# Gated units of a fused decoder kernel: token shift in the columns of the turned rows, with row statistics passed on by small transfers

## The chip, the core and the metric

The kernel is one launch on one core of a Trainium2 chip. Its metric is the device time of the launch in microseconds (us), lower is better. A core has a matrix engine (TensorE, PE in the views; its weight loads are PEld), a vector engine (VectorE, DVE), a scalar engine (ScalarE, ACT), a general engine (GpSimd, POOL) and a queue engine (SyncE, SP) that issues nearly all transfers of this kernel. Each engine takes its instructions in order and waits on semaphores for what other engines and transfers produce. A matmul contracts over the 128 partitions of its two operands in SBUF and writes to a bank of PSUM, which VectorE and ScalarE read.

## The reference, cut to what matters

A decoder of two layers on an input of 8 x 512 x 256 in float32: self-attention, cross-attention, a stage "ffn" of two local-attention layers with gated units, then quantised attention, media attention and experts. The change concerns the gated units, the second half of each of the two layers of the "ffn" stage:

```python
def shift_token(t):
    t1, t2 = jnp.split(t, 2, axis=-1)
    t2 = jnp.pad(t2, ((0, 0), (1, 0), (0, 0)))[:, :-1]
    return jnp.concatenate([t1, t2], axis=-1)
...
    x = x + o @ wo
    h = shift_token(x)
    mu = h.mean(-1, keepdims=True)
    var = h.var(-1, keepdims=True)
    h = (h - mu) / jnp.sqrt(var + 1e-05) * lg + lb
    h = h @ w1 + b1
    a, g = jnp.split(h, 2, axis=-1)
    h = a * jax.nn.gelu(g, approximate=False)
    x = x + h @ w2 + b2
```

So row t of h has channels 0 to 127 of row t and channels 128 to 255 of row t - 1 (zero for the first row of a sequence). The layer normalisation runs over this mixed row. The inner width of the unit is 682.

## The kernel before, in words

**Layout.** x stays in SBUF for the whole kernel as 128 partitions x 32 tiles x 256 channels. One of the 8 sequences ("block" b) is four tiles of 128 rows: row 128 i + p of the sequence lies in partition p of tile i. A shift by one row is therefore a shift by one partition, with a step from partition 127 of tile i - 1 to partition 0 of tile i.

**Stages and who puts them in order.** Each stage is a Python generator or function that records instructions. A generator of class Ahead yields between pieces of its preparation, and the stage before it calls ahead.step() in its last rounds, so that preparation of the next stage is recorded among them. local_attention (L1758) does so for local_ffn: one step at its start, one in each of its last seven rounds, and a last call that takes the rest up to "yield Ahead.MAIN". After recording, a scheduler puts the instructions of every engine in an order by their priority and by when it expects their inputs; it can move work ahead of what was recorded before it, within the limits of the tile pools (a tag with bufs=2 has two buffers, and a third user waits for the first to be released).

**local_ffn (L2015), before the change.** At its start it builds two 128 x 128 matrices, shift and carry (L2027 to L2031), by GpSimd selections: shift has ones where a column is the partition plus one, carry a single one from partition 127 to partition 0. Then, for a block:

- shifted(b), L2043: two matmuls (L2049 with shift, 512 columns, L2050 with carry, 384 columns) write the shifted upper channels of the four tiles to a bank; ScalarE copies it to lf_h (L2051). ln_stats (L134; L142, L143) runs BN statistics over the lower half of x and over lf_h, and one aggregation for the pair; rsqrt (L1455 to L1463) makes the inverse root in ten small VectorE instructions on 128 x 4 values. normalize (L154, L156) writes hn, eight instructions of 128 x 128.
- turned(b), L2060: eight PE transposes (L2066) put the channels on the partitions; VectorE scales each half with gain and bias of the layer normalisation from PSUM into hnT (L2069), 128 x 512 each.
- chunk(b, f), L2079, six times: matmuls with w1 for the gate and the other factor (up, L2073), Gelu on ScalarE (L2096, lf_gate), and the product on VectorE (L2100, lf_hid or lf_tail). The sixth chunk is the narrow tail.
- then, for each of four row tiles, six matmuls with w2 (L2143) and the sum into x (L2148). In the second layer GpSimd adds the residual (L2150) and finished(b) takes row statistics for the next stage.

Block 0's shifted, turned and chunks are recorded before MAIN, that is, in the end of local_attention. In the main part shifted(b + 1) is recorded at f = 0 of block b, turned(b + 1) at f = 3. Every matmul of float32 appears as two instructions in the trace, so the 2 of a shift are 4 rows.

**The neighbours.** The end of local_attention is a round trip: masks on VectorE (L1928, la_e), exponentials on ScalarE (L1932), products on PE (L1939, banks po and sum), a copy la_o (L1961, three buffers). The sums go to DRAM and back spread over the partitions (sums L3111, x_sums L3112), are inverted (L3115), go to DRAM (L3116) and come back wide (x_wide, L3128, four transfers); GpSimd multiplies (L3129, la_oT), and the output projection follows on PE (L1987) with the sum into x on VectorE (L1992). All of these transfers are issued by SP, in order.

Of the kernel before, what the change touches and what calls it, by code (L numbers as in the profile page):

```python
# [27 lines left out]
F32 = mybir.dt.float32  # L28
# [5 lines left out]
ALU = mybir.AluOpType  # L34
# [4 lines left out]
P = 128  # L39
B, S, C = 8, 512, 256  # L40
NST = S // P
NT = B * NST
EPS = 1e-5
# [12 lines left out]
class Decoder:  # L56
# [35 lines left out]
    def bank(self, tag):  # L92

        return self.alloc(self.psum, [P, 512], F32, tag)
# [1182 lines left out]
class FastDecoder(Decoder):  # L1277
# [737 lines left out]
    def local_ffn(self, l, y, ahead):  # L2015

        nc, t = self.nc, self.t
        w1, w2 = self.load_local_ffn(l)
        last = l == 1
        yield  # L2020
        with self.tc.tile_pool(
            name="lf", bufs=2, reuse_waits="tile", side="left" if last else "right"
        ) as pool:

            shift = self.alloc(pool, [P, P], F32, "lf_shift", bufs=1)
            carry = self.alloc(pool, [P, P], F32, "lf_carry", bufs=1)
            for m, step, base, mul in ((shift, 1, -1, -1), (carry, -P, 1 - P, 1)):  # L2027
                nc.gpsimd.affine_select(
                    out=m, in_=self.ones, pattern=[[step, P]], compare_op=ALU.is_equal, fill=0.0,
                    base=base, channel_multiplier=mul,  # L2030
                )  # L2031
            gb = self.alloc(pool, [P, 4], F32, "lf_gb", bufs=1)
            b1 = self.alloc(pool, [P, 2 * NHC - 1], F32, "lf_b1", bufs=1)
            nc.sync.dma_start(gb, t["c_ln"][l])
            nc.sync.dma_start(b1, t["c_b1"][l])

            tails = []
            for j in range(2):
                tails.append(self.alloc(pool, [64, S], F32, f"lf_tail{j}", bufs=1))
                nc.gpsimd.memset(tails[j][32:64, :], 1.0)  # L2040
            held = {}

            def shifted(b):  # L2043

                d = held[b] = {}
                h = self.alloc(pool, [P, NST, P], F32, "lf_h")
                ps = self.pj()
                rows = y[:, b * NST : (b + 1) * NST, :]
                nc.tensor.matmul(ps, shift, rows[:, :, P:], start=True, stop=False)  # L2049
                nc.tensor.matmul(ps[:, P:], carry, rows[:, : NST - 1, P:], start=False, stop=True)  # L2050
                nc.scalar.copy(h.rearrange("p t c -> p (t c)"), ps)  # L2051
                stats = self.ln_stats(pool, lambda i: [rows[:, i, :P], h[:, i, :]], NST, "lf_ln")
                hn = d["hn"] = self.alloc(pool, [P, NST, C], F32, "lf_hn")
                for i in range(NST):
                    self.normalize(hn[:, i, :P], rows[:, i, :P], stats, i)
                    self.normalize(hn[:, i, P:], h[:, i, :], stats, i)
                if last:
                    d["x"] = self.residual(pool, b)

            def turned(b):  # L2060
                d = held[b]
                hnT = d["hnT"] = self.alloc(pool, [P, 2, S], F32, "lf_hnT")
                for c in range(2):
                    ps = self.pj()
                    for i in range(NST):
                        nc.tensor.transpose(  # L2066
                            ps[:, i * P : (i + 1) * P], d["hn"][:, i, c * P : (c + 1) * P], self.ident
                        )
                    nc.vector.tensor_scalar(  # L2069
                        hnT[:, c, :], ps, gb[:, c : c + 1], gb[:, 2 + c : 3 + c], ALU.mult, ALU.add  # L2070
                    )

            def up(ps, b, at, m):  # L2073
                for k in range(2):
                    nc.tensor.matmul(  # L2075
                        ps[:m, :], w1[:, k, at : at + m], held[b]["hnT"][:, k, :], start=(k == 0), stop=(k == 1)
                    )

            def chunk(b, f, bank):  # L2079

                d = held[b]
                if f == 0:
                    d["hid"] = self.alloc(pool, [P, NHC - 1, S], F32, "lf_hid")
                last_f = f == NHC - 1
                m, at = (TAIL, 64) if last_f else (P, 0)
                pa = bank("sc")
                if last_f:
                    up(pa, b, 2 * (NHC - 1) * P, PAIR)
                    pg = pa
                else:  # L2090
                    pg = bank("pj")
                    up(pg, b, (NHC - 1 + f) * P, P)
                    up(pa, b, f * P, P)
                col = 2 * NHC - 2 if last_f else NHC - 1 + f
                gate = self.alloc(pool, [P, S], F32, "lf_gate")
                nc.scalar.activation(  # L2096
                    gate[:m, :], pg[at : at + m, :], AF.Gelu, bias=b1[at : at + m, col : col + 1]
                )
                col = 2 * NHC - 2 if last_f else f
                nc.vector.scalar_tensor_tensor(  # L2100
                    tails[b % 2][:m, :] if last_f else d["hid"][:, f, :],
                    pa[:m, :], b1[:m, col : col + 1], gate[:m, :], ALU.add, ALU.mult,
                )

            yield
            shifted(0)
            yield
            turned(0)
            for f in range(NHC):
                yield  # L2110
                chunk(0, f, lambda tag: self.pj())
            yield Ahead.MAIN
            with self.banks():
                self.pj = lambda: self.bank("tr")
                order = ("pj", "sc", "po", "tr") if last else ("sc", "tr", "pj", "po")
                self.reserve(self.psum, *((tag, [P, 512], 2) for tag in order))
                if last:
                    self.integers = ExitStack()
                    self.qpool = self.integers.enter_context(
                        self.tc.tile_pool(reuse_waits="tile", name="qw", bufs=1, side="right")  # L2120
                    )
                    self.q = {"stats": [], "xtop": self.alloc(self.qpool, [P, NT], F32, "qw_xtop")}
                    self.w_quantized = self.load_quantized_attention()
                ahead.step()
                for b in range(B):
                    for f in range(NHC):
                        if b:
                            chunk(b, f, self.bank)
                        if b + 1 < B:
                            if f == 0:  # L2130
                                shifted(b + 1)
                            if f == 3:
                                turned(b + 1)
                        if b >= B - 2:
                            ahead.step(2)
                    if last and b == 1:
                        self.integer_weights(self.qpool, self.w_quantized)
                    for i in range(NST):
                        ps = self.bank("po")
                        for f in range(NHC):  # L2140
                            last_f = f == NHC - 1
                            src = tails[b % 2][: TAIL + 1, :] if last_f else held[b]["hid"][:, f, :]
                            nc.tensor.matmul(  # L2143
                                ps[:, :C], src[:, i * P : (i + 1) * P], w2[: src.shape[0], f, :],
                                start=(f == 0), stop=last_f,
                            )
                        yt = y[:, b * NST + i, :]
                        nc.vector.tensor_tensor(yt, yt, ps[:, :C], ALU.add)  # L2148
                        if last:
                            nc.gpsimd.tensor_tensor(yt, held[b]["x"][:, i, :], yt, ALU.add)  # L2150
                    if last:
                        self.finished(b)
                ahead.step(100)
# [1232 lines left out]
```

## Time and profile before

| | us |
|---|---|
| median of 3 runs | 3223.38 (3217.72 to 3229.64) |
| the profiled execution | 3223.79 |
| its span in the trace | 3222.1 |
| PE matmul of the shift, L2049, one of 32 instructions (28 of them, 4 others 0.644) | 0.592 |
| PE matmul of the carry, L2050, one of 32 instructions | 0.486 |
| copies lf_h on ScalarE, L2051 (16 of 0.586), together | 9.4 |
| VectorE waits for x_sums (L3115, 23 of 78), together | 35.9 |

The profile is of one execution. In its page, section 2 cuts the span into 40 equal slices (80.6 us each), a digit being the busy share in tenths. Durations of matmuls are longer than the distance between their starts, since matmuls are pipelined: what an instruction costs on PE is read from start to start. In a timeline the columns are start, duration (of a merged group: from first start to last end), engine, line, operation, output and inputs, shapes and count; a bracket holds the idle time before and what ended it.

### The profile page before, as it was taken

The page shows a single profiled execution, that of the slowest core. Times are in us where ns is not written, and L with a number is a line of the kernel's source. Part 1 is how long each engine was busy: PE and PEld are TensorE (multiplying, and loading weights), DVE is VectorE, ACT ScalarE, POOL GpSimd, SP SyncE. Part 2 cuts the span into 40 slices and gives each one's busy share as a digit, 9 for nine tenths or more (in the row PEclk, how much of TensorE's full clock was granted, in tenths as well). Part 3 has the DMA queues.
Part 4 walks back from the last instruction along what each step waited for, and adds up shares of the span by engine and source line. Part 5 has one row for each costly group of instructions (what it writes and reads, how often), then busy time and mean ns, then how long its engine had stood idle before and what let it go on. Part 6 is the DMA issues. An engine that isn't in the chain of part 4 may idle for free. (4 is left out here: it accounts for less than half of the span.)

```text
span 3222.1 us, 40035 instructions
## 1 busy us (share of the span) xinstructions
PE 2949.9 (92%) x15008; PEld 1504.2 (47%) x15008; DVE 2143.2 (67%) x4766; ACT 1154.4 (36%) x1607; POOL 410.2 (13%) x383
## 2 busy tenths in 40 slices
PE   8998798878998999999988989999797899997998
PEld 5642222224554555555455546554444233333665
DVE  7458888887887854366788777656788866566110
ACT  2146566643434331123434431112255334442111
POOL 1111001000110110000011011011302122222111
PEclk9999999988999999999999999999898999998999
DMA  7011111101000000000000011001232122222431
GB/s 232 1 58 45 58 53 39 39 17 53 15 21 15 21 28 34 1 1 34 15 21 21 22 41 59 14 14 59 61 141 97 52 67 93 80 73 87 117 135 58
DMA packets 125921, 168.41 MB, mean 52 GB/s; under 512 B 47158, under 2 KB 74893, under 8 KB 123670
## 3 DMA queue, kind: packets, MB, share of 16 engines
q1 hardware_dynamic: 121622, 154.17, 14.9%
q0 software_dynamic: 4096, 11.59, 1.0%
q8 instruction: 120, 1.97, 0.3%
q14 instruction: 83, 0.68, 0.1%
HBM read 112.95 MB, written 47.50 MB: 50 GB/s over the span
## 5 line engine op out<-in xcount | busy, mean ns | idle before, releaser
L1811 PE MATMUL pj<-w,la_hT 128*128 128x512 f32 x720 | 348.6, 617 | 25.6 <-DVE la_v L1816 23.9
L1663 DVE TENSOR_TENSOR x_e<-x_e,x_share 128x1024 f32<-128x1024 f32 x256 | 307.1, 1245 | 24.0 <-ACT x_e L1662 23.2
L1662 ACT ACTIVATE x_e<-sc 128x1024 f32<-128x1024 f32 x256 | 249.7, 1026 | 145.2 <-PE sc L1651 143.6
L2758 ACT ACTIVATE ma_e<-sc,ma_bias 128x1024 f32<-128x1024 f32 x128 | 142.6, 1115 | 198.6 <-PE sc L2753 185.4
L1811 PEld LDWEIGHTS pj<-w,la_hT 128*128 128x128 f32 x720 | 130.3, 192 | 169.2 <-issue 120.0
L3129 POOL TENSOR_TENSOR la_oT<-la_o,x_wide 128x512 f32<-128x512 f32 x64 | 97.5, 1534 | 799.1 <-DMA x_wide<-invs 459.1
L1932 ACT ACTIVATE la_e<-la_e 128x1024 f32<-128x1024 f32 (+1 forms) x128 | 121.5, 951 | 184.0 <-DVE la_e L1928 184.0
L2096 ACT ACTIVATE lf_gate<-pj,lf_b 128x512 f32<-128x512 f32 (+1 forms) x82 | 56.4, 687 | 358.4 <-PE pj L2075 358.4
L2766 DVE TENSOR_TENSOR ma_esum<-ma_esum,ma_e 128x1024 f32<-128x1024 f32 x96 | 122.9, 1281 | 91.7 <-ACT ma_e L2758 91.1
L2075 PE MATMUL pj<-lf_hnT,w 128*128 128x512 f32 (+1 forms) x368 | 173.5, 598 | 0.0
L1678 PE MATMUL po<-x_e,x_v 128*32 128x512 f32 x1024 | 139.9, 619 | 36.2 <-DVE x_e L1663 32.9
L1928 DVE TENSOR_TENSOR la_e<-sc,la_mask 128x1024 f32<-128x1024 f32 (+1 forms) x128 | 138.4, 1082 | 44.5 <-PE sc L1921 44.5
L1651 PE MATMUL sc<-x_q,x_k 32*128 32x512 f32 x1024 | 158.3, 658 | 0.3 <-ACT x_e L1662 0.2
L2075 PE MATMUL sc<-lf_hnT,w 128*128 128x512 f32 x336 | 155.9, 592 | 0.0
L2143 PE MATMUL po<-w,lf_hid 128*128 128x256 f32 x640 | 153.9, 386 | 0.0
L2753 PE MATMUL sc<-ma_qT,ma_kT 64*128 64x512 f32 x512 | 144.9, 643 | 0.0
L1987 PE MATMUL pj<-w,la_oT 128*128 128x256 f32 x512 | 124.3, 389 | 21.7 <-ACT la_qkT L1857 12.6
L2776 PE MATMUL po<-ma_e,ma_v 128*64 128x512 f32 x512 | 138.1, 618 | 0.0
L1921 PE MATMUL sc<-la_qkT 64*128 64x256 f32 (+1 forms) x1024 | 135.8, 384 | 0.0
L2143 PEld LDWEIGHTS po<-w,lf_hid 128*128 128x128 f32 x640 | 117.3, 190 | 34.6 <-issue 20.4
L1939 PE MATMUL po<-la_e,la_v 128*64 128x256 f32 (+1 forms) x1024 | 129.2, 373 | 3.4 <-ACT la_o L1961 3.4
L1818 ACT ACTIVATE la_sq<-pj 128x512 f32<-128x512 f32 x120 | 71.5, 596 | 156.2 <-PE pj L1811 156.1
(491 smaller groups left out, 5233.9 us busy)
## 6 DMA issues: line engine op xcount, KB each, us to landing
x_wide<-invs SPq DMA_DIRECT2D x184, 128.0 KB
w<-in_f_w_dram SPq DMA_DIRECT2D x16, 1024.0 KB
kv<-kv_o SPq DMA_DIRECT2D x56, 256.0 KB
slots<-x_empty SPq DMA_DIRECT2D x8, 1028.0 KB
x_mask<-in_x_maskT_dram SPq DMA_DIRECT2D x8, 1024.0 KB
ma_kT<-kv SPq DMA_DIRECT2D x8, 1024.0 KB
ma_v<-kv SPq DMA_DIRECT2D x8, 1024.0 KB
ex_rows<-slots SPq DMA_DIRECT2D x7, 1028.0 KB
```

Source lines behind the costliest of these rows:

```text
L1651: nc.tensor.matmul(pair[r // 2][:, r % 2, :], d["k"][rows, g, kt * P : (kt + 1) * P], d["q"][rows, e, g, :], start=True, stop=True,)
L1662: nc.scalar.activation(ex, d["e"][rest][p], AF.Exp)
L1663: nc.vector.tensor_tensor(ex, ex, d["share"][:, kt, :].unsqueeze(1).broadcast_to([P, 2, 512]), ALU.mult)
L1678: nc.tensor.matmul(d["po"][32 * r : 32 * r + 32, :], d["v"][:, kt, 8 * g + 2 * r + e, :], ex[r // 2][:, r % 2, :], start=(kt == 0), stop=( ...
L1811: nc.tensor.matmul(ps, d["hT"][:, k, i * P : (i + 1) * P], wqkv[:, k, j * S : (j + 1) * S], start=(k == 0), stop=(k == 1),)
L1921: nc.tensor.matmul(ps[:, r, jj * 256 : jj * 256 + to - j * P], d["qkT"][rows, 4 + c, j * P : (j + 1) * P], d["qkT"][rows, c, j * P : to], ...
L1928: nc.vector.tensor_tensor(ex[:, :, :n_cols], ps[:, :, :n_cols], mask[:, :n_cols].unsqueeze(1).broadcast_to([P, 2, n_cols]), ALU.add,)
L2075: nc.tensor.matmul(ps[:m, :], w1[:, k, at : at + m], held[b]["hnT"][:, k, :], start=(k == 0), stop=(k == 1))
L2143: nc.tensor.matmul(ps[:, :C], src[:, i * P : (i + 1) * P], w2[: src.shape[0], f, :], start=(f == 0), stop=last_f,)
L2753: nc.tensor.matmul(ps[:, r, :], d["k"][rows, c, kt * P : (kt + 1) * P], d["q"][rows, c, :], start=True, stop=True,)
L2758: nc.scalar.activation(ex, ps, AF.Exp, bias=bias[:, b * NST + kt : b * NST + kt + 1], scale=0.125)
L2776: nc.tensor.matmul(d["po"][64 * r : 64 * r + 64, :], d["v"][:, kt, 128 * c + 64 * r : 128 * c + 64 * r + 64], ex[:, r, :], start=(kt == 0) ...
```

## The change

The shift moves from the rows to the columns. The rows of the lower and upper channels are normalised where they lie, unshifted, each with the scale and offset of the mixed row that it will belong to, and the upper half is shifted by one column when the turned rows are scaled out of PSUM into hnT. For that, statistics are taken for each half alone (two aggregations for what was one), the upper half's mean and variance are sent one partition on (before), both are combined to the mixed row's mean and variance, and the scale and offset of a row (own) are sent one partition back (next) for the upper half. Each of these is a pair of transfers from SBUF to SBUF, one of 127 partitions x 8 values and one that carries partition 127 to partition 0 or back. shifted(b) becomes three pieces, halves, scales and normal, recorded at f = 0, 1 and 2 of the block before, with turned at f = 4 rather than 3; for block 0 each piece has a yield.

```diff
-            shift = self.alloc(pool, [P, P], F32, "lf_shift", bufs=1)
-            carry = self.alloc(pool, [P, P], F32, "lf_carry", bufs=1)
-            for m, step, base, mul in ((shift, 1, -1, -1), (carry, -P, 1 - P, 1)):
-                nc.gpsimd.affine_select(
...
+            befores, owns, nexts = [], [], []
+            for j in range(2):
+                befores.append(self.alloc(pool, [P, NST, 2], F32, f"lf_before{j}", bufs=1))
+                nc.gpsimd.memset(befores[j], 0.0)
+                owns.append(self.alloc(pool, [P, NST + 1, 2], F32, f"lf_own{j}", bufs=1))
+                nc.gpsimd.memset(owns[j], 0.0)
+                nexts.append(self.alloc(pool, [P, NST, 2], F32, f"lf_next{j}", bufs=1))
             held = {}
 
-            def shifted(b):
+            def halves(b):
 
                 d = held[b] = {}
-                h = self.alloc(pool, [P, NST, P], F32, "lf_h")
-                ps = self.pj()
-                rows = y[:, b * NST : (b + 1) * NST, :]
-                nc.tensor.matmul(ps, shift, rows[:, :, P:], start=True, stop=False)
-                nc.tensor.matmul(ps[:, P:], carry, rows[:, : NST - 1, P:], start=False, stop=True)
-                nc.scalar.copy(h.rearrange("p t c -> p (t c)"), ps)
-                stats = self.ln_stats(pool, lambda i: [rows[:, i, :P], h[:, i, :]], NST, "lf_ln")
+                rows = d["rows"] = y[:, b * NST : (b + 1) * NST, :]
+                mv = d["mv"] = self.alloc(pool, [P, 2, NST, 2], F32, "lf_mv")
+                for j in (1, 0):
+                    for i in range(NST):
+                        st = self.alloc(pool, [P, 6], F32, "lf_bn", bufs=4)
+                        nc.vector.bn_stats(st, rows[:, i, j * P : (j + 1) * P])
+                        nc.vector.bn_aggr(mv[:, j, i, :], st)
+                    if j:
+                        before = befores[b % 2]
+                        nc.sync.dma_start(before[1:], mv[: P - 1, 1])
+                        nc.sync.dma_start(before[0:1, 1:], mv[P - 1 :, 1, : NST - 1])
+
+            def scales(b):
+
+                mv, before, own, next_ = held[b]["mv"], befores[b % 2], owns[b % 2], nexts[b % 2]
+                total = self.alloc(pool, [P, NST, 2], F32, "lf_total")
+                apart = self.alloc(pool, [P, NST], F32, "lf_apart")
+                rstd = self.alloc(pool, [P, NST], F32, "lf_rstd")
+                nc.vector.tensor_tensor(total, mv[:, 0], before, ALU.add)
+                nc.vector.tensor_tensor(apart, mv[:, 0, :, 0], before[:, :, 0], ALU.subtract)
+                nc.vector.scalar_tensor_tensor(apart, apart, 0.5, apart, ALU.mult, ALU.mult)
+                nc.vector.tensor_tensor(apart, apart, total[:, :, 1], ALU.add)
+                nc.vector.tensor_scalar(apart, apart, 0.5, EPS, ALU.mult, ALU.add)
+                self.rsqrt(pool, rstd, apart, "lf_t")
+                nc.vector.tensor_copy(own[:, :NST, 0], rstd)
+                nc.vector.scalar_tensor_tensor(
+                    own[:, :NST, 1], total[:, :, 0], -0.5, rstd, ALU.mult, ALU.mult
+                )
+                nc.vector.tensor_copy(own[:, NST, 1:2], own[:, 0, 1:2])
+                nc.sync.dma_start(next_[: P - 1], own[1:, :NST])
+                nc.sync.dma_start(next_[P - 1 :], own[0:1, 1:])
+
+            def normal(b):
+                d = held[b]
                 hn = d["hn"] = self.alloc(pool, [P, NST, C], F32, "lf_hn")
-                for i in range(NST):
-                    self.normalize(hn[:, i, :P], rows[:, i, :P], stats, i)
-                    self.normalize(hn[:, i, P:], h[:, i, :], stats, i)
+                for j, (part, to) in enumerate(((slice(0, P), owns), (slice(P, C), nexts))):
+                    for i in range(NST):
+                        to_ = to[b % 2][:, i]
+                        nc.vector.tensor_scalar(
+                            hn[:, i, part], d["rows"][:, i, part], to_[:, 0:1], to_[:, 1:2],
+                            ALU.mult, ALU.add,
+                        )
...
-                    nc.vector.tensor_scalar(
-                        hnT[:, c, :], ps, gb[:, c : c + 1], gb[:, 2 + c : 3 + c], ALU.mult, ALU.add
-                    )
+                    pieces = (((0, S), (0, S)),) if c == 0 else (((1, S), (0, S - 1)), ((0, 1), (S - 1, S)))
+                    for (lo, hi), (lo_, hi_) in pieces:
+                        nc.vector.tensor_scalar(
+                            hnT[:, c, lo:hi], ps[:, lo_:hi_], gb[:, c : c + 1], gb[:, 2 + c : 3 + c],
+                            ALU.mult, ALU.add,
+                        )
...
             yield
-            shifted(0)
+            halves(0)
+            yield
+            scales(0)
+            yield
+            normal(0)
             yield
             turned(0)
...
-                            if f == 0:
-                                shifted(b + 1)
-                            if f == 3:
-                                turned(b + 1)
+                            if f in (0, 1, 2, 4):
+                                (halves, scales, normal, None, turned)[f](b + 1)
```

In the built program VectorE has 11 instructions more for each of the 16 blocks, SP 64 transfers more in all, PE and ScalarE have the shift's matmuls and copies fewer, and the orders of the engines differ from the first local attention's end on to the end of the second layer's gated units. What is recorded after that stands in the same order on PE.

More of the change, by code (lines that the diff above doesn't have):

```diff
@@ L2023, in local_ffn @@
         ) as pool:
-            shift = self.alloc(pool, [P, P], F32, "lf_shift", bufs=1)
-            carry = self.alloc(pool, [P, P], F32, "lf_carry", bufs=1)
-            for m, step, base, mul in ((shift, 1, -1, -1), (carry, -P, 1 - P, 1)):
-                nc.gpsimd.affine_select(
-                    out=m, in_=self.ones, pattern=[[step, P]], compare_op=ALU.is_equal, fill=0.0,
-                    base=base, channel_multiplier=mul,
-                )
             gb = self.alloc(pool, [P, 4], F32, "lf_gb", bufs=1)
@@ L2068, in turned @@
                         )
-                    nc.vector.tensor_scalar(
-                        hnT[:, c, :], ps, gb[:, c : c + 1], gb[:, 2 + c : 3 + c], ALU.mult, ALU.add
-                    )
+                    pieces = (((0, S), (0, S)),) if c == 0 else (((1, S), (0, S - 1)), ((0, 1), (S - 1, S)))
[4 more added lines that the diff above has]
+                        )
             def up(ps, b, at, m):
```

## The prediction

> **What bounds the kernel now.** I read the page first (shares, then the slices), then a table of windows cut at the stage borders, then the timeline of TensorE, VectorE and SP in those windows.
>
> ```profile
> PE 2949.9 (92%) x15008; PEld 1504.2 (47%) x15008; DVE 2143.2 (67%) x4766; ACT 1154.4 (36%) x1607; POOL 410.2 (13%) x383
> PE   8998798878998999999988989999797899997998
> DVE  7458888887887854366788777656788866566110
> ...
> 1140.00:1201.00 61.00, 55.85 (x334) 28.76 (x333) 33.66 (x70) 19.74 (x27) 10.23 (x10) 0.92 0.11 32
> 1201.00:1216.00 15.00, 14.90 (x67) 12.36 (x66) 4.09 (x9) 0.68 (x1) 2.54 (x3) 1.00 0.00 1
> 1216.00:1400.00 184.00, 184.00 (x590) 103.19 (x590) 76.21 (x272) 24.81 (x37) 0.00 (x0) 1.00 0.05 15
> 1880.00:1939.00 59.00, 53.22 (x334) 27.52 (x333) 33.93 (x70) 19.67 (x27) 10.14 (x10) 0.97 0.16 50
> 1954.00:2180.00 226.00, 225.35 (x736) 126.72 (x735) 150.05 (x539) 30.20 (x45) 24.26 (x31) 1.00 0.10 31
> ```
>
> Columns of the windows: stretch, its length, busy us (count) of PE, PEld, DVE, ACT, POOL, then granted clock, DMA share, GB/s. Seen over the whole span PE is only 92% busy, but in the two gated-unit stages (1216 to 1400, 1954 to 2180) it is busy without a gap at full clock, while VectorE is at 41% and 66%. In those stages a PE instruction removed is time removed. In the ends of the two local attentions before them (1140 to 1201, 1880 to 1939) PE stands 5.2 and 5.8 us.
>
> The timeline of one block of rows:
>
> ```profile
> 1266.28 1.02 PE L2049 MATMUL tr<-x,lf_shift 128*128 128x512 f32 x2
> ...
> 1297.76 1.88 PE L2075 MATMUL sc<-lf_hnT,w 128*128 128x512 f32 x4
> 1299.47 1.02 PE L2049 MATMUL tr<-x,lf_shift 128*128 128x512 f32 x2
> 1300.33 0.81 PE L2050 MATMUL tr<-x,lf_carry 128*128 128x384 f32 x2
> 1300.98 1.88 PE L2075 MATMUL pj<-lf_hnT,w 128*128 128x512 f32 x4
> ```
>
> Start to start (durations overlap in the pipeline): the shift takes 1299.47 to 1300.33, the carry to 1300.98, together 1.51 us; the period of a block is 1299.47 - 1266.28 = 33.19 us, all of it PE. That is the part that the change removes.
>
> At the attention's end the block's first rows are on the path instead:
>
> ```profile
> 1164.21 0.49 DVE L142 BATCH_NORM_STATS2 lf_ln_bn<-lf_h 128x6 f32<-128x128 f32 x2 [2.10 <-ACT lf_h L2051]
> 1173.36 1.22 DVE L1928 TENSOR_TENSOR la_e<-sc,la_mask 128x1024 f32<-128x1024 f32 x1
> ...
> 1168.30 1.08 PE L1939 MATMUL po<-la_e,la_v 128*64 128x256 f32 x8 [0.38 <-ACT la_o L1961]
> 1171.70 1.63 PE L2066 MATMUL pj<-ident,lf_hn 128*128 128x128 f32 x5 [2.31 <-DVE lf_hn L156]
> ...
> 1170.24 0.52 SPq L3111 DMA_DIRECT2D sums<-la_total  x1
> 1171.94 0.32 SPq L3112 DMA_DIRECT2D x_sums<-sums  x1
> ```
>
> PE waits 2.31 us for the normalised rows (2.26 in two waits in layer 1). Two SP lines give the price of a small transfer: x_sums waits for sums, 1171.94 - 1170.24 - 0.52 = 1.2 us after its issue ended, so some 1.7 us from issue to landing.
>
> **What the Trainium skill says.** "DMA: Bandwidth & Descriptors", section "Anatomy of one DMA", gives about 2.0 us fixed per transfer, most of it the write receipt; the 1.7 us above agrees, though that page fits another issuing path. "VectorE: DVE Perf Modes", section "The TRN2 errata", says that operands read from SBUF cost a fixed extra per instruction; the trace shows it, 0.15 to 0.16 us for four elements per partition. "SBUF — State Buffer", section "SBUF: two separate sides", says of the port pair shared by VectorE and GpSimd that it is an exclusive lock. This fits L148 at 1166.41, 1.25 us long instead of 0.16 beside a GpSimd product.
>
> **The change part by part.**
>
> *Removed, TensorE.* 16 blocks (8 rows of the batch, 2 layers), each shift and carry: 16 x 1.51 = 24.2 us. Of these 14 lie in the windows with a solid PE (21.1 us, taken in full) and 2 in the attention ends (3.0 us).
>
> *Removed, ScalarE.* 16 copies of 0.586 us (L2051). ScalarE is 13% busy in the stage: nothing, except that in the attention end the chain matmul, copy, statistics becomes statistics alone.
>
> *VectorE, per block.* Before: 8 BN statistics, 4 aggregations, 2 copies, 10 of the root, 8 normalisations, 2 turned scalings. After: 8, 8, 5 sums, 10, 3 for own, 8, 3 scalings. So 4 aggregations (0.192 us), 6 small ones (0.155) and the one-column piece (0.15, by the small ones) more: 1.85 us, 30 us in all. In the solid stages this lies in VectorE's idle time (59% and 34%). The one tight place there is the order transposes, scalings, normalisations, tail product: by starts, 0.9 us for the transposes, 1.72 for the last up matmuls and 2.25 for five down matmuls leave 4.85 us; VectorE needs 0.8 + 2 x 0.75 + 0.1 + 4 x 0.26 + 0.66 = 4.1. It fits, with 0.7 to spare.
>
> *Transfers.* Four per block on SP, 64 in all, about 0.35 us of issue each (x_sums' 0.32), 22 us of an idle queue. Two waits per block are added on VectorE: the sums wait for before, the second half of the normalisation for next. In the built order of instructions next is issued a block ahead of its use in the stages, some 30 us for a transfer of 1.7; so the price there is 0. Behind a wait stand masks, exponent inputs and gate products on VectorE, so it is not 0 in the attention ends.
>
> *Moved.* Since the statistics no longer need TensorE, the built order puts those of blocks 1 to 6 (7's too, in part) into the attention's end and the up matmuls beside it. Chunks of block 0 also start two steps later, since the preparation has two yields more; they still stand ahead of the output projection and fill the same wait. Between two gate products VectorE now has about 6 statistics pairs (0.26 us, start to start), 16 small ones (0.06 to 0.2 apart, I take 0.12) and the product (0.66): 4.1 us against 3.43 us of PE for a chunk. Over four chunks and two layers that is at most 5.6 us; the two banks take up part, and I charge 3. On SP the wide copies of the inverse sums now queue behind transfers that wait for VectorE, in layer 1 also behind four bias loads (about 0.45 us each by L2204's issues). I follow this by hand to 3 to 5 us later for the first pair; la_o has three buffers, so PE can wait there (0.38 before). Against it stand the 2.31 and 2.26 us waits that go, and masks that come up to 4 us earlier because the copy is gone. These bounds are -4 (gain) to +8 (loss) over both ends; I take +2 less the 3.0 for the removed pair, so the two ends together gain 1.
>
> *Setup.* Two selections per layer go, four memsets come (0.49 us each at most, on an idle GpSimd): 0.
>
> Sum: 21.1 + 1 = 22 us. The profiled execution took 3223.79 us (span 3222.1), less 22 gives 3201.8; the median shown is 0.4 lower. I say **3202**.
>
> **The rivals.**
>
> *A, VectorE takes over the attention ends* (chance 0.20). The gate products come late in each of the eight chunks, by up to 0.7 + 0.5 us of small operations spaced 0.15 apart, and two or three small-transfer waits fall on VectorE at the mean of the 23 waits that L3115 has now (35.9 / 23 = 1.56 us). For: six blocks of 8 pairs (2.1 us) and 18 small ones (2.2) are 26 us of new VectorE work there, in windows with 27 and 25 us idle. Against: most of it is placed where VectorE now waits for PE. Loss 10 us more: 3212, inside the uncertainty.
>
> *B, slower: SP's order holds up the attention's end* (0.07). A transfer on SP waits for VectorE's own; the wide copies of the inverses stand behind it; so GpSimd's product, the la_o buffers and PE wait, and with them the masks. Three rounds in each of two ends; the gain is eaten from 3.7 us a round (22 / 6), and slower by 0.5% from 6.4. At 7 us a round: 3223.8 - 22 + 42 = 3244. Against: each round has VectorE's own within 1 to 2 us of the queue reaching it in my walk, and output projections of the block before give 7.2 us of cover.
>
> *C, more gain* (0.08): the ends profit too, by both waits and earlier masks, 4 to 7 us more: 3196.
>
> *D, the shift's time isn't PE's* (0.05): removed matmuls leave gaps because the bank or gate chain sets the pace. A chunk's gate starts 0.2 us after its matmuls and PE shows no wait in 184 us, so I don't expect it; half the gain, 3213.
>
> **How the numbers follow.** The forecast has 0.60, with its own range 3197 to 3207. The range for 8 in 10 takes in most of A and D and part of C: 3195 to 3215. A measurement of this kernel tells about 0.5% (16 us) from no change: below 3207.3 counts as faster. Faster: 0.60 + 0.08 and a part of A and D, 0.72; same 0.21; slower 0.07.
>
> **What would show it.** L2049, L2050 and L2051 gone, the block's period 31.7 instead of 33.2 us, PE without a gap from the output projection on. A shows as PE idle before up matmuls released by lf_hid in the ends; B as PE released by la_o or by la_oT, with SP waiting on own before wide copies. Wrong if the periods don't fall by 1.5 us, or if the two ends together are longer by over 5 us than now.

## The result and the profile after

The changed kernel takes 3199.13 us in the median of 5 runs (3188.31 to 3200.42), the kernel before 3223.92 (3217.72 to 3229.64) in the runs beside it: a ratio of 0.9921, 95% interval 0.9904 to 0.9939. The forecast of 3202 stands for 0.9934, the range of 3195 to 3215 holds the median. The profiled execution took 3199.13 us, with a span of 3197.2.

The page's first section, after:

```profile
PE 2931.4 (92%) x14944; PEld 1489.4 (47%) x14944; DVE 2156.5 (67%) x4942; ACT 1144.1 (36%) x1591; POOL 405.8 (13%) x387
```

The shares are the same as before; TensorE has 64 rows fewer, VectorE 176 more. Where the time went is in the stages. I cut both traces at the same events: an end runs from the last matmuls of the last but one output projection (L1987) to the first of the last one, a stretch from there to the last row tile's down matmuls of the last block (L2143, now L2182). The columns are as in the prediction's windows. Before:

```profile
1130.38:1201.06 70.68, 65.53 (x380) 34.49 (x377) 41.40 (x85) 24.12 (x34) 10.23 (x10) 0.93 0.11 32
1201.06:1482.22 281.16, 280.98 (x917) 159.25 (x915) 130.95 (x399) 47.59 (x76) 4.13 (x9) 1.00 0.03 10
1870.33:1939.08 68.75, 62.97 (x381) 33.24 (x378) 41.72 (x85) 24.10 (x34) 10.14 (x10) 0.98 0.16 48
1939.08:2199.55 260.47, 259.73 (x861) 149.95 (x859) 159.18 (x557) 33.63 (x50) 28.21 (x35) 1.00 0.09 27
```

After:

```profile
1129.46:1196.61 67.15, 58.92 (x376) 31.53 (x373) 62.71 (x264) 23.49 (x33) 8.82 (x12) 1.00 0.13 35
1196.61:1468.27 271.66, 270.38 (x889) 154.29 (x887) 115.55 (x309) 43.57 (x69) 4.12 (x9) 1.00 0.03 11
1853.32:1925.08 71.76, 64.54 (x376) 32.99 (x373) 61.65 (x274) 23.83 (x34) 9.24 (x12) 0.93 0.19 54
1925.08:2173.60 248.52, 248.42 (x832) 145.03 (x833) 145.70 (x457) 29.07 (x43) 28.43 (x35) 1.00 0.08 26
```

The stretches are 9.50 and 11.95 us shorter, 21.45 together. The ends went from 139.43 to 138.91, 0.52 less, at clocks that differ (0.93 and 0.98 before, 1.00 and 0.93 after). The local attention of the second layer between them, which the change doesn't touch, reads 388.11 before and 385.05 after; over the twelve further profiles below it lies between 382.3 and 388.3, so its 3.06 are spread. What comes ahead of the first end is 0.92 shorter, what follows the last stretch 1.05 longer. Together: 0.92 + 0.52 + 9.50 + 3.06 + 11.95 - 1.05 = 24.9 us, the difference of the two spans.

The block's period, in the timeline of TensorE in the second stretch: first two blocks of before, then two of after (each line is the first down matmuls of a block):

```profile
2093.53 2.32 PE L2143 MATMUL po<-w,lf_hid 128*128 128x256 f32 x10
...
2126.71 2.32 PE L2143 MATMUL po<-w,lf_hid 128*128 128x256 f32 x10
```

```profile
2038.90 2.32 PE L2182 MATMUL po<-w,lf_hid 128*128 128x256 f32 x10
...
2070.58 2.32 PE L2182 MATMUL po<-w,lf_hid 128*128 128x256 f32 x10
```

33.18 before, 31.68 after: the 1.5 us of the two matmuls. The waits of TensorE in the two ends of after (the bracket names the idle time and what ended it):

```profile
1167.61 1.73 PE L1939 MATMUL po<-la_e,la_v 128*64 128x256 f32 x16 [2.73 <-ACT la_o L1961]
1171.12 0.33 PE L2100 MATMUL pj<-ident,lf_hn 128*128 128x128 f32 x1 [0.86 <-DVE lf_hn L2087]
1183.60 1.98 PE L2112 MATMUL pj<-lf_hnT,w 128*128 128x512 f32 x4 [0.74 <-ACT lf_gate L2133]
1186.05 10.72 PE L2112 MATMUL pj<-lf_hnT,w 128*128 128x512 f32 x24 [0.47 <-DVE lf_hid L2137]
...
1872.21 1.16 PE L1854 MATMUL pj<-ident,la_qk 128*128 128x128 f32 x8 [2.79 <-DVE la_qk L1845]
...
1894.57 0.48 PE L2100 MATMUL pj<-ident,lf_hn 128*128 128x128 f32 x1 [2.52 <-DVE lf_hn L2087]
...
1914.03 10.57 PE L2112 MATMUL pj<-lf_hnT,w 128*128 128x512 f32 x24 [0.67 <-DVE lf_hid L2137]
1925.08 14.42 PE L1987 MATMUL pj<-w,la_oT 128*128 128x256 f32 x64 [0.48 <-DVE lf_t L1461]
```

Before, TensorE stood 10.93 us in the two ends (length less busy time), after 15.45. The waits for the first block's rows did not go: a wait for la_o of 2.73 us takes the place of 0.38 in the first end, and lf_hn still costs 2.52 in the second.

### The profile page after: what moved, and what is told of

Read it like the earlier page. It is cut to its first block, busy times and chain, and to the rows that moved or that the text cites. A ratio compares the mean times of both kernels' runs of the same rounds, so it can differ in the third digit from the quotient of the medians.

```text
span 3197.2 us, 40205 instructions
## 1 busy us (share of the span) xinstructions
PE 2931.4 (92%) x14944; PEld 1489.4 (47%) x14944; DVE 2156.5 (67%) x4942; ACT 1144.1 (36%) x1591; POOL 405.8 (13%) x387
## 3 DMA queue, kind: packets, MB, share of 16 engines
q8 instruction: 119, 1.95, 0.3%
## 5 line engine op out<-in xcount | busy, mean ns | idle before, releaser
L1928 DVE TENSOR_TENSOR la_e<-sc,la_mask 128x1024 f32<-128x1024 f32 (+1 forms) x128 | 138.6, 1083 | 40.5 <-PE sc L1921 40.5
L2182 PE MATMUL po<-w,lf_hid 128*128 128x256 f32 x640 | 153.5, 387 | 0.0
L1987 PE MATMUL pj<-w,la_oT 128*128 128x256 f32 x512 | 124.2, 389 | 23.4 <-ACT la_qkT L1857 12.6
L2137 DVE SCALAR_TENSOR_TENSOR lf_hid<-sc,lf_b,lf_gate 128x512 f32<-128x512 f32 x70 | 52.5, 750 | 135.3 <-PE sc L2112 135.3
L2182 PEld LDWEIGHTS po<-w,lf_hid 128*128 128x128 f32 x640 | 117.4, 190 | 34.8 <-issue 20.7
```

The source lines that it names most:

```text
L1928: nc.vector.tensor_tensor(ex[:, :, :n_cols], ps[:, :, :n_cols], mask[:, :n_cols].unsqueeze(1).broadcast_to([P, 2, n_cols]), ALU.add,)
L2182: nc.tensor.matmul(ps[:, :C], src[:, i * P : (i + 1) * P], w2[: src.shape[0], f, :], start=(f == 0), stop=last_f,)
```

## The experiments

All times are medians, each beside runs of the kernel before. "Ends" and "stretches" are the sums of the two stages of each kind in one profile, "idle" is TensorE's in the ends.

| run | us | ratio to before, 95% interval | ends | idle | stretches |
|---|---|---|---|---|---|
| before (profile) | 3223.92 | | 139.43 | 10.93 | 541.63 |
| changed kernel (profile) | 3199.13 | 0.9921 (0.9904 to 0.9939) | 138.91 | 15.45 | 520.18 |
| again | 3200.05 | 0.9935 (0.9918 to 0.9951) | 137.18 | 13.01 | 520.17 |
| twice | 3241.01 | 1.0059 (1.0043 to 1.0076) | 136.07 | 9.91 | 563.56 |
| bare | 3198.61 | 0.9928 (0.9911 to 0.9945) | 132.48 | 12.62 | 519.53 |
| still | 3198.53 | 0.9924 (0.9906 to 0.9942) | 135.10 | 14.02 | 519.81 |
| late | 3211.11 | 0.9965 (0.9954 to 0.9976) | 135.71 | 15.21 | 532.92 |
| latepack | 3203.16 | 0.9947 (0.9930 to 0.9965) | 129.92 | 11.29 | 532.74 |
| pool_queue | 3208.89 | 0.9962 (0.9948 to 0.9976) | 140.76 | 18.30 | 520.19 |
| f3 | 3196.09 | 0.9917 (0.9897 to 0.9936) | 138.38 | 14.23 | 519.35 |
| pack | 3200.87 | 0.9924 (0.9910 to 0.9938) | 137.17 | 13.79 | 520.74 |
| packf3 | 3202.13 | 0.9930 (0.9917 to 0.9942) | 141.26 | 13.35 | 520.58 |
| best | 3209.66 | 0.9948 (0.9932 to 0.9964) | 134.39 | 11.54 | 531.53 |
| next | 3192.08 | 0.9914 (0.9896 to 0.9931) | 132.54 | 12.23 | 519.80 |

### Is it the matmuls? again, twice, bare

The changed kernel once more:

> The changed kernel once more, as the neighbour of the next three. Theory (the shift's matmuls were TensorE time, and the rest of the change costs some microseconds in the two attention ends): ratio to before 0.990 to 0.994, period of a block in the solid stretch 31.7 us. Chance (part of the gain was the luck of that one comparison): ratio 0.995 or more. In the ends I expect TensorE idle again 7 to 8 us each, against 5.2 and 5.8 in the kernel before.

The gain repeats (0.9935). The idle of 6.20 and 6.81 us in the two ends is less than I expected.

The kernel before with the shift done twice:

```diff
-                nc.tensor.matmul(ps, shift, rows[:, :, P:], start=True, stop=False)
-                nc.tensor.matmul(ps[:, P:], carry, rows[:, : NST - 1, P:], start=False, stop=True)
+                for _ in range(2):
+                    nc.tensor.matmul(ps, shift, rows[:, :, P:], start=True, stop=False)
+                    nc.tensor.matmul(ps[:, P:], carry, rows[:, : NST - 1, P:], start=False, stop=True)
```

> The kernel before with each shift and carry matmul done twice (the same values twice into the same bank). Theory: 16 x 1.51 = 24 us more, ratio 1.0075, block period 34.7 us. Rival (removed or added shift time is only partly TensorE's, the gate chain takes part of it): 12 us more or less, ratio under 1.004, period under 34.0.

18.8 us more (3241.01 - 3222.24; the interval of the ratio is 14 to 24 us, with the expected 24 at its edge). The first stretch of twice,

```profile
1202.85:1494.54 291.69, 291.50 (x945) 164.57 (x943) 130.96 (x399) 47.59 (x76) 4.14 (x9) 1.00 0.03 10
```

grew by 10.53 us (291.69 against 281.16), which is 7 blocks of 1.50; the second by 11.40, of which 1.16 are further waits of TensorE. The total is less than these 21.9 us because the ends (136.07 against 139.43) and the attention between (384.84 against 388.11) came out shorter. What the two added pairs cost there can't be read against before: TensorE's clock was 1.00 in both ends here, 0.93 and 0.98 before. So a pair costs 1.5 us in a stretch, and rival D falls.

The kernel before with the shift left out:

```diff
-                h = self.alloc(pool, [P, NST, P], F32, "lf_h")
-                ps = self.pj()
...
-                nc.tensor.matmul(ps, shift, rows[:, :, P:], start=True, stop=False)
-                nc.tensor.matmul(ps[:, P:], carry, rows[:, : NST - 1, P:], start=False, stop=True)
-                nc.scalar.copy(h.rearrange("p t c -> p (t c)"), ps)
-                stats = self.ln_stats(pool, lambda i: [rows[:, i, :P], h[:, i, :]], NST, "lf_ln")
+                stats = self.ln_stats(pool, lambda i: [rows[:, i, :P], rows[:, i, P:]], NST, "lf_ln")
...
-                    self.normalize(hn[:, i, P:], h[:, i, :], stats, i)
+                    self.normalize(hn[:, i, P:], rows[:, i, P:], stats, i)
```

> The kernel before without the shift: matmuls and copy gone, statistics and normalisation read the upper channels unshifted (the token shift is left out). No new VectorE work, no transfers, no early statistics. Theory: 24 us of TensorE and some 2 us of the wait for the first rows less, 3197 to 3200, so within 3 us of the changed kernel, and TensorE idle in each end under 5 us. Rival (the gain of the change comes from its early statistics and the order it brings, not from the matmuls): bare stays above 3207, some 8 us or more behind the changed kernel.

3198.61, within 1.5 us of the changed kernel (3200.05 in the same comparison): what the change adds costs nothing that this can tell (each interval reaches some 5 us to either side). But the expected idle of under 5 us an end was wrong. Even with nothing added TensorE stands 6.62 and 6.00 us there, together 1.7 more than before, and its waits for la_o are 1.47 and 1.95 us, against 0.38 and 0.57 before. I read this as the attention's own round trip setting part of the pace in the ends. Twice and bare, whose clocks in the ends are alike (1.00 and 1.00; 1.00 and 0.97), differ there by four pairs, 6.0 us of matmuls: the ends of bare are 3.6 us shorter and its idle is 2.7 us longer. So TensorE work taken out in an end partly becomes waiting, and partly is a gain.

### What the ends wait for: still, pool_queue, pack

The changed kernel without its transfers, each partition using its own statistics and scales (the exchange between rows is left out):

```diff
-                        before = befores[b % 2]
-                        nc.sync.dma_start(before[1:], mv[: P - 1, 1])
-                        nc.sync.dma_start(before[0:1, 1:], mv[P - 1 :, 1, : NST - 1])
...
-                mv, before, own, next_ = held[b]["mv"], befores[b % 2], owns[b % 2], nexts[b % 2]
+                mv, own = held[b]["mv"], owns[b % 2]
+                before = mv[:, 1]
...
-                nc.sync.dma_start(next_[: P - 1], own[1:, :NST])
-                nc.sync.dma_start(next_[P - 1 :], own[0:1, 1:])
...
-                for j, (part, to) in enumerate(((slice(0, P), owns), (slice(P, C), nexts))):
+                for j, (part, to) in enumerate(((slice(0, P), owns), (slice(P, C), owns))):
```

> The changed kernel without its 64 small transfers: the upper half's statistics and scales are used in their own partition (the exchange between partitions is left out), VectorE's work unchanged. If the waits added in the ends come from the transfers (SP's order, wait for next): TensorE idle falls from 8.2 and 7.2 us to about 5 to 6 in each end, 3 to 5 us less in all than the changed kernel. If they come from VectorE's early statistics alone: idle stays at 7 to 8 us and the time within 2 us of the changed kernel.

Idle 14.02 and a median 1.5 us below again's: the transfers are not what the ends wait for. In their absence no wait of TensorE for lf_hn is left in the ends, but its waits for la_o are 2.80 and 3.80 us: one wait of the round trip took over from another. Moved to GpSimd's queue (`nc.gpsimd.dma_start` for the four `nc.sync.dma_start` of halves and scales):

> The changed kernel with the 64 small transfers issued by GpSimd's queue in place of SP's, nothing else. If SP's order is what holds up la_o and la_oT (rival B's mechanism): the waits for la_o in the ends (2.7 us in the first end) go to under 1 us, 3 us less in all. If VectorE is: idle in the ends stays at 13 to 15 us. A loss is possible from GpSimd's own order: products wait behind a transfer that waits for own.

Idle rose to 18.30 and the median by 8.8 us against again (the two intervals just meet), with la_o waits of 3.28 and 3.69 us. By itself this doesn't clear SP's order, since GpSimd's queue also makes la_oT and its products may now stand behind transfers; together with still it does. Of the loss, 5.3 us are idle in the ends; the stage after the last stretch was also 5.6 us longer (1028.76 against 1023.17), which the edit doesn't touch and which I leave open.

Then the suspicion that block 0's chunks come too late, since its preparation has two steps more:

```diff
             halves(0)
-            yield
             scales(0)
-            yield
             normal(0)
```

> The changed kernel with one edit: halves, scales and normal of block 0 are recorded in one piece, so its chunks come two steps of the attention earlier, as many steps as before the change. The early statistics of later blocks stay. If the two added steps make the ends' waits: idle of the two ends together falls from 13.0 to 15.5 us to 11.5 or less and their length from 137 to 139 us by 3 to 6; the time 3 to 5 us less than the changed kernel, some 3195. If the early statistics make them: idle stays 13 or more, the time within 2 us of the changed kernel. The stretches keep 271.7 and 248.5 us.

Idle 13.79, the same time: alone, the two steps cost nothing, as the prediction had it, and the suspicion is not borne out.

### What the early statistics are for: late, latepack, f3, packf3, best, next

late holds the statistics of blocks 1 to 7 behind the newest VectorE instruction recorded, so that they leave the end:

```diff
+                                if f == 0:
+                                    with self.tc.issue_after(next(
+                                        i for i in reversed(self.nc.cur_bb.bb.instructions)
+                                        if i.engine == mybir.EngineType.DVE
+                                    )):
+                                        halves(b + 1)
+                                else:
+                                    (None, scales, normal, None, turned)[f](b + 1)
-                                (halves, scales, normal, None, turned)[f](b + 1)
```

> The changed kernel with the statistics of blocks 1 to 7 held back behind the newest gate product, so that none of them falls into the attention's end. If VectorE's early statistics make the ends' waits: idle in the two ends together falls from 13 to 15.5 us (two profiles) to 11 or less, as before (10.9), and the waits for lf_hid and lf_rstd or lf_t before up matmuls and output projection go; time 2 to 4 us less than the changed kernel, about 3196. If SP's order makes them: also less idle, so the next but one must tell. If neither: idle stays at 13 and over. The solid stretch keeps its period of 31.7 us in every case.

The opposite of what I expected: some 10 us slower than the changed kernel by the ratios (the intervals of late and again don't meet), and the idle in the ends is no less. The period didn't grow in every block: in the first stretch it is 31.68 us from block 2 on, as in the changed kernel, and only the step from block 0 to block 1 takes 37.37; in the second that step takes 40.92 in place of 33.33. There the statistics come only after the output projection: in the first stretch they start at 1212.5, the rows are wanted at 1226.0, and the chain from statistics to rows took 17.1 us. latepack (late and pack together):

> As late, and the first block's halves, scales and normal are recorded in one piece, two steps of the attention earlier. If the end is bound by the first block's chain (statistics, exchange, rows, transposes): TensorE's waits for lf_hn and lf_hnT in the end go, some 2 us less than late. If the end is bound by the attention itself (la_qk, la_o): the same as late within 1 us of idle.

Its ends are the shortest of all (129.92), and its stretches lose 12.6 us, as late's lose 12.7. So whatever the early statistics cost the ends, those of block 1 are also the cover of its transfers. In the ends the two edits act together: late and pack alone leave the idle at 15.21 and 13.79 us, where the changed kernel has 15.45 and 13.01; with both it is 11.29 here, and 11.54 and 12.23 in best and next below. These are single profiles. In between, f3 (turned recorded at f = 3 in place of 4) and packf3:

> The changed kernel with the turned rows at f = 3, as before, in place of f = 4. Theory: in the solid stretches nothing, period 31.7 us; the one wait of 1.18 us for lf_hnT in block 7 of layer 0 goes, since the last up matmuls give VectorE one chunk more. Rival (the tight order at f = 4 costs in every block): 3 us or more less than the changed kernel. Within 2 us of the changed kernel by mine.

> Pack and f3 together: the two gains add, since one lies in the ends and the other in block 7 of layer 0 (270.9 us in place of 271.7): 1 us less than pack, some 3194, ratio to before about 0.991.

f3 does what it should in its place: the timeline of the changed kernel has one wait in the first stretch, at the transposes of block 7, where the next attention's first matmuls share the bank with the transposes,

```profile
1411.95 1.98 PE L1811 MATMUL tr<-w,la_hT 128*128 128x512 f32 x4 [1.18 <-DVE lf_hnT L2105]
```

and f3's first stretch is 270.87 us in place of 271.66. In the time this can't be told. packf3's sum did not appear: its median is no lower than pack's.

best is packf3 with the statistics of blocks 2 to 7 held back in late's way (`if f == 0 and b:`), block 1's free:

> Packf3, and the statistics of blocks 2 to 7 held back behind the newest gate product; block 1's stay free, since in late the stretches lost 5.5 and 8.4 us where block 1's came after the output projection. If the early statistics cost something in the ends besides the two steps: ends as in latepack (65.1 and 64.8 us) and stretches as in f3 (270.9 and 248.5 us), together 8 us less than the changed kernel, 3191 to 3193, ratio 0.990. If they cost nothing: the same as packf3 within 1.5 us, or slower, if a block's own statistics then come late (a period over 31.7 us).

Its median is 7.5 us above packf3's; the two intervals overlap, but the stretches are 11 us longer, and the trace shows where. VectorE and then TensorE in best, around the preparation of block 2 (the line numbers are the changed kernel's up to L2137):

```profile
1239.78 0.17 DVE L2067 TENSOR_TENSOR lf_total<-lf_mv,lf_before 128x8 f32<-128x8 f32 x1 [0.92 <-DMA lf_before<-lf_mv]
...
1243.44 0.14 DVE L2077 COPY lf_own<-lf_own 128x1 f32<-128x1 f32 x1
...
1247.27 1.11 DVE L2087 TENSOR_SCALAR lf_hn<-x,lf_next 128x128 f32<-128x128 f32 x4 [2.66 <-DMA lf_next<-lf_own]
```

```profile
1247.76 0.75 PE L2100 MATMUL tr<-ident,lf_hn 128*128 128x128 f32 x3 [2.45 <-DVE lf_hn L2087]
```

The statistics start after the first gate product (1234.68), the rows are wanted after the fourth chunk; two transfers in a row with VectorE's in-order work between them don't fit, and TensorE stands 2.45 us in the middle of the stretch. The blocks after it in the first stretch have a period of 32.7 us in place of 31.68. Of the 11 us, 4.3 are further waits of TensorE; in the rest it counts as busy, with its transposes (L2100) taking 23.6 us in place of 14.6.

That late, which holds the statistics back in the same way, has no such loss from block 2 of the first stretch on shows how much cover is needed. VectorE and then TensorE in late, block 3:

```profile
1266.33 0.48 DVE L2054 BATCH_NORM_STATS2 lf_bn<-x 128x6 f32<-128x128 f32 x2
1276.37 1.11 DVE L2087 TENSOR_SCALAR lf_hn<-x,lf_next 128x128 f32<-128x128 f32 x4 [0.86 <-DMA lf_next<-lf_own]
1279.12 1.04 PE L2100 MATMUL tr<-ident,lf_hn 128*128 128x128 f32 x8
```

From the first statistics (1266.33) to the last row (1277.48) the chain takes 11.2 us, in the same block of best too. The turned rows at f = 4, after the fifth chunk, leave it 12.8 us here, and the eight transposes run without a wait; at f = 3 they leave 9.4 in best. A chunk more was enough, not a whole block.

next keeps f = 3 and gives back the cover by hand: statistics a block ahead, each held behind a gate product, so that 16 pairs and not 48 lie in the end.

```diff
+            def behind(b):
+                with self.tc.issue_after(next(
+                    i for i in reversed(self.nc.cur_bb.bb.instructions)
+                    if i.engine == mybir.EngineType.DVE
+                )):
+                    halves(b)
...
                 chunk(0, f, lambda tag: self.pj())
+                if f == 1:
+                    behind(1)
+                if f == 2:
+                    scales(1)
...
-                        if b + 1 < B:
-                            if f in (0, 1, 2, 3):
-                                (halves, scales, normal, turned)[f](b + 1)
+                        if f < 2 and b + 2 < B:
+                            (behind, scales)[f](b + 2)
+                        if f in (2, 3) and b + 1 < B:
+                            (normal, turned)[f - 2](b + 1)
```

> Packf3 with the statistics held back and moved a block ahead by hand: block 1's behind the second gate product of block 0, block b+2's behind the first gate product of block b, so that each transfer still has a block's time and only 16 of the early statistics pairs, not 48, lie in the attention's end. If the stretches stay solid only because the transfers are issued a block ahead (in best VectorE waited 2.66 us for next and TensorE 2.45): stretches 270.9 and 248.5 us again, in place of 277.7 and 253.8. If the early statistics then still cost the ends: ends 130 to 135 us together in place of 137 to 141, the time 3 to 6 us less than packf3, 3196 or less, ratio 0.991. If the stretches are lost again: 3205 or more.

Windows of next, the same four stages:

```profile
1128.74:1195.89 67.15, 60.78 (x377) 32.27 (x373) 46.87 (x134) 26.17 (x35) 8.74 (x12) 0.97 0.10 26
1195.89:1466.76 270.87, 270.54 (x890) 154.03 (x888) 134.93 (x438) 43.59 (x69) 4.12 (x9) 1.00 0.04 13
1849.08:1914.47 65.39, 59.53 (x376) 31.60 (x373) 46.85 (x134) 25.96 (x35) 9.25 (x12) 1.00 0.18 51
1914.47:2163.40 248.93, 248.52 (x834) 144.63 (x832) 159.91 (x596) 29.53 (x43) 28.23 (x35) 1.00 0.09 28
```

The stretches are solid again, 519.80 in place of best's 531.53 (0.9914 against 0.9948; the intervals don't overlap). The second transfer is not issued a block ahead here: in 14 of 16 blocks its second half goes out 1.8 to 2.7 us before VectorE uses it. What came earlier is the chain as a whole. VectorE has 47 us of work in an end in place of 61. The ends are 132.54 us in place of 141.26 (packf3), but most of that is TensorE's clock (0.97 and 1.00 against 0.98 and 0.91), and the idle differs by 1.1 us only: what the early statistics cost the ends stays unresolved, between 1 us and that difference. At 3192.08 next has the lowest median, but its ratio's interval overlaps the changed kernel's: that it beats it isn't shown.

## Why the prediction was right

**Removed, TensorE.** 21.1 us were put in the solid stretches; they shrank by 21.45. The period fell by 1.50, and twice and bare confirm the price from both sides. The second stretch gave 11.95, more than its 7 x 1.51 = 10.6; in part this is two waits for lf_hn (0.40 and 0.18) that the kernel before had there and that went with the copy. The first gave 9.50, less than 10.6, for the wait of 1.18.

**VectorE.** "It fits, with 0.7 to spare" held at all transposes but those of block 7 in the first layer (1.18 us), where I hadn't looked at who shares the bank.

**Transfers.** The price of 0 in the stretches was right, and that a cover makes it 0 was too: best shows the price without it, 2.66 us on VectorE and 2.45 on TensorE in one block. But the cover was described too narrowly, as next issued a block ahead: the stretches of next are solid with that transfer issued just before its use, and late's first stretch is from block 2 on, with the whole chain inside one block. The issue cost was mis-sized: I took 0.35 us from x_sums; the four have medians of 0.64 to 0.77, 16 x (0.642 + 0.767 + 0.718 + 0.648) = 44 us of SP in place of 22. In the stretches TensorE shows no wait for it.

**Moved.** The ends were to gain 1 and gained 0.52, but not by the terms of the sum, and that the two numbers lie close is luck: one half-clock cell fewer in the ends (see the last section), some 1.7 us, is more than the whole 0.52. The waits of 2.31 and 2.26 us for the first block's rows were to go: in the first end 0.86 remain ahead of the transposes and 0.30 ahead of the up matmuls, and la_o took the rest's place (2.73), in the second lf_hn alone costs 0.23 + 0.53 + 2.52. For the last, SP's timeline of after shows how:

```profile
1886.56 0.43 SPq L2243 DMA_DIRECT2D qw_bias<-in_d_bo_dram  x1
1887.10 0.37 SPq L3155 DMA_DIRECT2D invs<-x_inv  x1
1887.90 0.70 SPq L2059 DMA_DIRECT2D lf_before<-lf_mv  x1
1889.08 0.66 SPq L2058 DMA_DIRECT2D lf_before<-lf_mv  x1
1890.91 0.49 SPq L3167 DMA_DIRECT2D x_wide<-invs  x1
1891.49 0.61 SPq L2078 DMA_DIRECT2D lf_next<-lf_own  x1
1892.20 0.84 SPq L2079 DMA_DIRECT2D lf_next<-lf_own  x1
```

own was written by 1890.04; next went out behind a wide copy, its second half at 1892.20, and the normalisation ran at 1894.16, after a mask (L1928) and 0.77 us of VectorE waiting for next. The idle rose by 4.5 us (2.1 in again); 1.7 of it bare shows too, with nothing added. Gate products came late by 0.47 and 0.67 us: rival A's mechanism, at about a tenth of its 10 us. Rival B did not come: idle in still shows that the ends as a whole don't hang on SP. Nor did C: no 4 to 7 us came from the ends.

So the forecast was right because the term that carried it, 14 pairs at 1.51 us in stretches with a solid TensorE, was read from start to start where TensorE sets the end. That term is shown; the term for the ends was too small to decide anything.

## What to carry to other kernels

Where an engine is busy without a gap at full clock, price removed work from start to start in that stage, and expect only part of that price where the engine waits for a round trip (3.6 us for 6.0 of matmuls here). A chain of small transfers is free as long as its whole length, with the in-order work between, fits before the place where its result is wanted (11.2 us here: it fitted 12.8 and not 9.4). Look for what the scheduler put early, and before tidying it away ask which latency it covers. A wait that shrinks can hand its time to the next one in the same round trip (lf_hn to la_o in still).

## What the runs showed of the hardware

After some waits TensorE ran at half clock for whole multiples of 3.41 us, at points of one fixed grid. In the second end of the changed kernel, cut on that grid:

```profile
1866.43:1869.84 3.41, 2.99 (x14) 1.30 (x12) 3.41 (x4) 0.72 (x2) 1.83 (x2) 1.00 0.00 0
1869.84:1873.26 3.42, 1.05 (x8) 0.83 (x8) 3.39 (x4) 1.09 (x2) 1.21 (x6) 1.00 0.05 2
1873.26:1876.67 3.41, 3.41 (x18) 1.95 (x16) 0.54 (x1) 1.69 (x3) 0.00 (x0) 0.50 0.00 0
1876.67:1880.08 3.41, 3.41 (x50) 2.11 (x48) 3.19 (x15) 1.33 (x2) 0.00 (x0) 1.00 0.38 113
...
1890.33:1893.74 3.41, 1.17 (x4) 0.55 (x4) 3.06 (x10) 0.31 (x1) 0.00 (x0) 1.00 0.15 41
1893.74:1897.15 3.41, 2.58 (x15) 0.99 (x19) 2.70 (x6) 0.74 (x1) 0.49 (x1) 0.50 0.39 119
1897.15:1900.57 3.42, 3.42 (x25) 1.22 (x17) 1.15 (x3) 1.33 (x2) 2.05 (x2) 0.50 0.03 6
1900.57:1903.98 3.41, 3.41 (x30) 1.66 (x30) 2.39 (x21) 1.52 (x2) 0.00 (x0) 1.00 0.04 5
```

A cell in which TensorE was busy 31% (1.05 of 3.42) or 34% is followed by cells at 0.50, and the clock comes back after a cell that was full. The Trainium skill, page "TensorE: Matmul & The Clock Gate", section "Part 1: The HAM clock gate (the "warmup" mystery)", describes such a grid: a free-running window of 3413 ns, half clock after an idle window, full clock after a busy one. The grid agrees: in each of the 14 traces all stretches of half clock start within 1 ns of one grid of 3413 ns. But a window didn't have to be idle: a third busy was too little. I counted the cells of the 14 traces, from 10 us into each span on: all 328 cells at full clock with TensorE busy under 40% are followed by half clock, 3 of the 11204 with 65% or more, and 114 of the 692 between. Worked out from these lines, a full cell at 0.50 costs half its time, 1.7 us, on top of the wait; a wait of about the same length, 2.68 us in next, cost nothing of the kind (its end has a clock of 1.00). It fell across two cells, busy 69% and 53%:

```profile
1862.82:1866.24 3.42, 2.36 (x12) 0.91 (x10) 3.42 (x3) 0.91 (x2) 1.08 (x1) 1.00 0.00 0
1866.24:1869.65 3.41, 1.79 (x15) 1.32 (x16) 3.17 (x4) 1.13 (x3) 1.21 (x6) 1.00 0.05 2
```

My reading is that where a wait falls on the grid decides it. The counts bear this out, though no run was made to move a wait along the grid. The ends of packf3 hold five cells at half clock and those of next one: of the 8.7 us between them some 7 are these cells. The ends of before hold four, those of the changed kernel three, and again's four. So I don't read the sums of the ends more finely than some 5 us.
